# A planner's numbers in a Strassen-like MoE kernel: landing time of two weight loads, rank of the reads of one PSUM bank

## The chip, the core and the metric

The kernel runs on one core of a Trainium2 chip. The metric is the device time of one execution in microseconds. Before the change, three runs took 2589.47, 2592.99 and 2593.93 us; the median is 2592.99 us.

## The reference

Sixteen sequences of 256 tokens with 256 features go through a mixture of experts with a residual. All is float32.

```python
# x (16, 256, 256); E = 8 experts, D = 256, F = 1024; p (16, 8) gating, s (16,) shared gate
g = einsum('bsd,edf->ebsf', x, Wg)
u = einsum('bsd,edf->ebsf', x, Wu)
expert_outs = einsum('ebsf,efd->ebsd', silu(g) * u, Wd)
expert_output = einsum('be,ebsd->bsd', p, expert_outs)
shared = einsum('bsf,fd->bsd', silu(x @ Sg) * (x @ Su), Sd)
out = x + (1 - s) * expert_output + s * shared
```

Every token goes through every expert: the gating only weighs. The shared expert is treated as a ninth one.

## The kernel before

The work is cut into 72 units: nine experts, two halves of the hidden size F, and four groups `g` of four sequences each. Units follow one another with the group as the inner loop, so a half of an expert's weights serves four units in a row, and new weights are needed once in four units.

A unit has two parts. `unit_up` makes gate and up projections with fewer multiplications than the plain product: four sequences and four chunks of weights are combined. For each of the two matrices (m = 0 gate, m = 1 up) there are "diagonal" products, made by `diagonal`, and six "off-diagonal" ones, made by `offdiagonal`. `unit_down` makes the down projection of the unit from seven products in PSUM banks `dn`, and adds them to DRAM tensors `total` through accumulating DMAs that POOL issues (L743). The `h` sums that those products read are made by the helper `sum_` in `unit_down`: two or three on DVE, and one, o3 = `a[0,0] - a[1,0]`, on POOL.

The steps of `diagonal`, on the single PSUM bank D: two matmuls (`ps`), a copy of the bank to `p_` on ACT (L536), two more matmuls into the same bank (`qs`), two DVE subtractions `q_ = bank - p_` (the reads of the bank, shown as `pq<-D,pq`), and then `consume`: for the gate an ACT silu into `sg` (L607), for the up matrix a DVE multiplication into `h` (`h<-D,coef,sg`, L273). Only then is the bank free for the next diagonal.

The steps of `offdiagonal`: POOL makes `s` from `p_` and `q_` (`s<-pq,pq`), TensorE makes one product in a bank M, DVE adds both and so seeds both halves of a bank X (`X<-M,s`), TensorE adds two products to it (`X<-xp,wp`), and gate or up consumes it. There are three X banks, two M banks, three `s` tiles.

Weights: `load_base` loads 256 KB and again 256 KB of gate or up weights into one tile `wb` (two halves, `u` and `v`), and then makes in its second half combinations of the two: two on POOL (`wb<-wb`, L268), one on DVE (L273). `make_pair` makes from them the tiles `wp` on POOL and DVE. There are four `wb` tiles, two of which each half of an expert needs.

Other inputs: in the first four units, `make_xd` and `make_xp` transpose and combine x into tiles `xd` and `xp` and keep them in DRAM; later units load them from there on SP's queue. In the last units, `finish` combines the `total` parts, transposes them back (L829), adds x and stores.

What sets the order. Nothing is written down in the order in which it runs. Each step is given to a `Plan` with an engine, an estimated length, a rank, its predecessors, and a `lag`: how long after its end others can use the result (0.25 where nothing else is given). `Plan.run` goes through a planned time: on each engine it takes, of the steps whose predecessors have ended and lagged, the one of the lowest rank that can have its buffers; TensorE alone must keep to the rank order. It also hands out the buffers, from a queue of free ones per kind, in planned time. When all is planned, the steps are emitted in that order, and the tile layer below builds the program for each engine's queue from it, with the semaphores. Ranks are counted in units of W = 12 per unit of work; r0 is the rank at which a unit starts.

A load's lag is 3 + KB/150 us unless it is given. For `load_base`, `lag` is given except in the first unit (rank below 0): that is line L291, and `u` and `v` both have it, `v` being planned after `u`. The down weights have 12 as well; they are not touched.

Of the kernel before, what the change touches and what calls it, by code (L numbers as in the profile page):

```python
# [46 lines left out]
class Plan:  # L47
# [18 lines left out]
    def add(self, engine, length, rank, emit, deps=(), new=(), uses=(), lag=None):  # L66
        lag = self.HOP if lag is None else lag
        op = Op(engine, length, lag, rank, emit, deps, list(new), list(uses))
        for b in [*op.new, *op.uses]:
            b.users += 1  # L70
        self.ops.append(op)
        return op
# [77 lines left out]
def kernel(  # L150
# [72 lines left out]
    def act(n):  # L223
        return 0.13 + n * 0.0009
# [38 lines left out]
    def load(rank, dst, src, kb, deps=(), new=(), uses=(), lag=None):  # L263
        return add("SP", 0.6, rank, lambda: nc.sync.dma_start(dst(), src), deps, new, uses, lag=lag or 3 + kb / 150)  # L264

    def tt(engine, rank, o, a, b, op, n, deps, new=(), uses=(), slow=1.0):
        eng, length = (nc.vector, dve(n) * slow) if engine == "DVE" else (nc.gpsimd, pool(n))
        return add(engine, length, rank, lambda: eng.tensor_tensor(o(), a(), b(), op), deps, new, uses)  # L268

    def stt(rank, o, a, c, b, op, n, deps, new=(), uses=(), more=0.0):  # L270
        return add(
            "DVE", dve(n, True) + more, rank,
            lambda: nc.vector.scalar_tensor_tensor(o(), a(), c() if callable(c) else c, b(), ALU.mult, op),  # L273
            deps, new, uses,
        )


    def sources(e):
        return (Wg[e], Wu[e], Wd[e]) if e < E else (Sg, Su, Sd)
# [5 lines left out]
    def load_base(m, e, half, rank):  # L285
        b = Buf("wb", f"wb_{m}_{e}_{half}")
        src = [
            sources(e)[m][ts(part, P), ts(half, 4 * P)].rearrange("p (c q) -> p c q", q=P)
            for part in range(2)
        ]  # L290
        lag = None if rank < 0 else 12  # L291
        u = load(rank, lambda: b[:, :, 0, :], src[0], 256, [], [b], lag=lag)
        v = load(rank, lambda: b[:, :, 1, :], src[1], 256, [u], [], [b], lag=lag)
        ops = []
        for i, t in enumerate(POINTS):
            r, x_ = (lambda i=i: b[:, i, 1, :]), (lambda i=i: b[:, i, 0, :])
            if t == 0:
                op = v
            elif abs(t) == 1:
                op = tt("POOL", rank + 1, r, r, x_, ALU.add if t > 0 else ALU.subtract, P, [u, v], uses=[b])  # L300
            else:
                op = stt(rank + 1, r, x_, float(t), r, ALU.add, P, [u, v], uses=[b])
            ops.append(op)
        base[m, e, half], baseop[m, e, half] = b, (u, ops)
# [201 lines left out]
    def mm(length, rank, o, w, mv, start, stop, onto, deps, new=(), uses=()):  # L506
        return add(
            "PE", length, rank,
            lambda: nc.tensor.matmul(o(), w(), mv(), start=start, stop=stop, skip_group_check=onto),  # L509
            deps, new, uses,  # L510
        )
# [3 lines left out]
    def diagonal(n, m, unit, a, rank, pq, consume):  # L515

        e, half, g = unit
        w, (u, rops) = base[m, e, half], baseop[m, e, half]
        xb, xo = xd[g, a], xdop[g, a]
        name = f"{m}_{n}_{a}"  # L520
        bank = Buf("D", f"D_{name}")
        p_, q_ = pq
        new = a == 0
        ps, qs = [], []
        for h, i in enumerate((2 * a + 1, 2 * a)):
            ps.append(
                mm(
                    MM, rank + 1 / 8 + h / 100, lambda h=h: bank[:, h, :], lambda i=i: w[:, i, 0, :],
                    lambda i=i: xb[:, i % 2, :], h == 0, True, h == 1, [u, xo[i][0], *ps],
                    [bank] if h == 0 else [], [w, xb] if h == 0 else [w, xb, bank],  # L530
                )
            )

        sp = add(
            "ACT", act(2 * TB), rank + 0.3,
            lambda: nc.scalar.copy(p_[:, 2 - 2 * a : 4 - 2 * a, :], bank[:, :, :]), ps,  # L536
            [p_] if new else [], [bank] if new else [bank, p_],
        )
        for h, i in enumerate((2 * a + 1, 2 * a)):
            qs.append(  # L540
                mm(
                    MM, rank + 9 / 8 + h / 100, lambda h=h: bank[:, h, :], lambda i=i: w[:, i, 1, :],
                    lambda i=i: xb[:, 2 + i % 2, :], False, True, True, [rops[i], xo[i][1], sp],
                    [], [w, xb, bank],
                )
            )
        ops = {}
        for h, i in enumerate((2 * a + 1, 2 * a)):
            first = new and h == 0
            ops[i] = tt(  # L550
                "DVE", rank + 1.5, lambda i=i: q_[:, i, :], lambda h=h: bank[:, h, :],
                lambda i=i: p_[:, 3 - i, :], ALU.subtract, TB, [*qs, *ops.values()],
                [q_] if first else [], [bank, p_] if first else [bank, p_, q_],
            )
        consume(bank, [*ops.values()], rank + 1.6, [(2 * a + 1, 2 * a + 1), (2 * a, 2 * a)])
        return ops

    def offdiagonal(n, m, unit, k, rank, pq, pqops, consume):
# [31 lines left out]
    def unit_up(n, unit):  # L590
# [70 lines left out]
        for d in range(4):  # L661
            a, m = d // 2, d % 2
            pqops[m].update(
                diagonal(n, m, unit, a, r0 - W + 3 * d, pqs[m], (gate, mult)[m](f"d{a}"))
            )
# [215 lines left out]
    for n, unit in enumerate(units):  # L881
        e, half, g = unit
        r0 = W * n
        if g == 0:
            for m in range(2):
                load_base(m, e, half, r0 - W + 3 * m - (8 if n else 4))
                if n == 0 and m == 0:
                    first_raw = load_raw(-12.5)
            for k in range(len(PAIRS)):
                for m in range(2):  # L890
                    make_pair(m, e, half, k, r0 + 2 * k + m - (8 if n else -4))
            load_down(e, half, r0 + W - 8)
# [63 lines left out]
```

## Time and profile before

| what | value |
|---|---|
| median of three runs | 2592.99 us |
| the profiled execution | 2590.57 us |
| its span in the profile | 2588.8 us |
| granted TensorE clock, mean | 0.997 |
| TensorE busy | 2525.8 us, 98% |
| VectorE (DVE), GpSimd (POOL), ScalarE (ACT) busy | 1846.1, 1800.1, 788.8 us |
| DMA | 421.47 MB, 163 GB/s |
| chain that ended last: TensorE, DMA, DVE | 88%, 6%, 3% of the span |
| wb loads of Wg, issue to landing (median, 33 of them) | 5.5 us |

How to read it. Times are microseconds from the start of the span. A row of a timeline has start, duration, engine, line, operation and tiles (written tile first); in brackets is how long the engine stood idle ahead of it, and what ended that. A row of the waits has who waited for whom: total, times, longest. Almost all operations are recorded through helpers, so that one line (L268 for two-input adds, L273 for multiply-adds, L509 for matmuls) stands for many steps; the tiles tell them apart. TensorE's busy time has modelled ends.

### The profile page before, as it was taken

To read this page: it belongs to the slowest core of one execution; us is meant where nothing else is said; L and a number is where in the kernel's file an instruction comes from. 1 tells how busy PE (TensorE), PEld (TensorE's weight loads), DVE (VectorE), ACT (ScalarE), POOL (GpSimd) and SP (SyncE) were. 2 spreads that over 40 slices of the span, in tenths; PEclk is the share of its full clock that TensorE was granted. 3 is DMA by queue.
4 is the path that set the end of the run, shared out by engine and by line. 5 is a ranking of instruction groups with operands and counts; after the bars stand their busy time and mean duration, and the time that the engine had idled before them with its cause. 6 is when DMAs were issued, how large, how long until landed. Compare 5 with 4: busy or idle time off the path is not lost.

```text
span 2588.8 us, 30164 instructions
## 1 busy us (share of the span) xinstructions
PE 2525.8 (98%) x9644; PEld 1819.9 (70%) x9644; DVE 1846.1 (71%) x3272; ACT 788.8 (30%) x1367; POOL 1800.1 (70%) x1638
## 2 busy tenths in 40 slices
PE   8899999999999999999999999999999999999998
PEld 4667777767776777777676767777776777677766
DVE  6886766777676767676677767676766667776797
ACT  2333333333333333333333333333332333333310
POOL 5686767667676767676766757686767677676654
PEclk9999999999999999999999999999999999999999
DMA  6545666656666656666665665665666666666652
GB/s 196 197 162 154 171 157 164 162 158 164 166 157 164 157 158 169 154 170 156 163 161 161 161 166 157 167 154 158 171 154 164 161 165 158 163 163 177 174 188 90
DMA packets 179087, 421.47 MB, mean 163 GB/s; under 512 B 15057, under 2 KB 84193, under 8 KB 170225
## 3 DMA queue, kind: packets, MB, share of 16 engines
q1 hardware_dynamic: 159280, 294.70, 34.4%
q0 software_dynamic: 19648, 124.86, 26.2%
q8 instruction: 75, 1.23, 0.2%
q14 instruction: 84, 0.68, 0.1%
HBM read 276.90 MB, written 142.61 MB: 162 GB/s over the span
## 4 chain that ended last, share of the span: by engine, by line
PE 88%; DMA 6%; DVE 3%; issue 1%; POOL 1%; SPq 0%; ACT 0%; DVEq 0%; POOLq 0%
PE dn L509 31%; PE X L509 27%; PE D L509 17%; PE M L509 14%; DMA wb<-in_L_cond_Wg_dram 4%; DVE h L273 1%; DMA wb<-in_L_cond_Sg_dram 1%; DVE X L268 1%; DVE h L268 1%; SPq L264 0%; DMA total<-ev 0%; POOL wp L268 0%; PE dn L829 0%; DVE xp L268 0%; DMA wb<-in_L_cond_Wu_dram 0%
## 5 line engine op out<-in xcount | busy, mean ns | idle before, releaser
L268 POOL TENSOR_TENSOR s<-pq,pq 128x512 f32<-128x512 f32 x852 | 1191.3, 1402 | 483.2 <-DVE X L268 471.8
L509 PE MATMUL dn<-h,wd 128*128 128x512 f32 x1988 | 1018.0, 594 | 1.4 <-DVE xd L273 1.4
L509 PE MATMUL X<-xp,wp 128*128 128x256 f32 x3408 | 878.2, 380 | 37.0 <-DVE X L268 37.0
L268 DVE TENSOR_TENSOR X<-M,s 128x512 f32<-128x512 f32 x852 | 586.7, 692 | 435.4 <-PE M L509 227.9
L509 PEld LDWEIGHTS X<-xp,wp 128*128 128x128 f32 x3408 | 645.7, 190 | 254.5 <-issue 103.4
L509 PE MATMUL D<-xd,wb 128*128 128x256 f32 x2272 | 584.5, 380 | 2.6 <-ACT pq L536 2.2
L509 PEld LDWEIGHTS M<-xp,wp 128*128 128x128 f32 x1704 | 324.4, 190 | 346.0 <-issue 338.2
L509 PE MATMUL M<-xp,wp 128*128 128x256 f32 x1704 | 508.1, 380 | 0.1
L729 ACT COPY ev<-dn 128x512 f32<-128x512 f32 x476 | 278.8, 586 | 708.6 <-PE dn L509 708.6
L509 PEld LDWEIGHTS D<-xd,wb 128*128 128x128 f32 x2272 | 431.5, 190 | 67.3 <-ACT pq L536 3.9
L273 DVE SCALAR_TENSOR_TENSOR h<-X,coef,sg 128x256 f32<-128x256 f32 x852 | 375.9, 475 | 122.2 <-PE X L509 107.8
L268 DVE TENSOR_TENSOR h<-h,h 128x512 f32<-128x512 f32 x426 | 448.0, 1052 | 1.9
L509 PEld LDWEIGHTS dn<-h,wd 128*128 128x128 f32 x1988 | 377.6, 190 | 54.8 <-DVE xd L273 2.2
L607 ACT ACTIVATE sg<-X 128x512 f32<-128x512 f32 x434 | 259.1, 597 | 441.8 <-PE X L509 278.0
L536 ACT COPY pq<-D 128x512 f32<-128x512 f32 x284 | 166.5, 586 | 501.7 <-PE D L509 498.3
L268 DVE TENSOR_TENSOR pq<-D,pq 128x256 f32<-128x256 f32 x568 | 218.9, 416 | 25.5 <-PE D L509 25.3
L268 POOL TENSOR_TENSOR h<-h,h 128x512 f32<-128x512 f32 x142 | 197.8, 1393 | 3.6 <-DVE h L268 2.9
L743 POOL DMA_DIRECT2D total<-ev x128 | 112.8, 881 | 66.4 <-ACT ev L729 63.7
L268 POOL TENSOR_TENSOR wb<-wb 128x128 f32<-128x128 f32 x72 | 48.5, 684 | 129.1 <-DMA wb<-in_L_cond_Wg_dram 98.0
L273 DVE SCALAR_TENSOR_TENSOR h<-D,coef,sg 128x256 f32<-128x256 f32 x284 | 134.8, 475 | 0.0
L273 DVE SCALAR_TENSOR_TENSOR wp<-wb,wp 128x256 f32<-128x256 f32 x108 | 106.6, 998 | 29.9 <-POOL wp L268 24.0
L607 ACT ACTIVATE sg<-D 128x512 f32<-128x512 f32 x142 | 84.4, 594 | 98.5 <-DVE pq L268 98.5
(68 smaller groups left out, 561.1 us busy)
## 6 DMA issues: line engine op xcount, KB each, us to landing
xp<-keep_p SPq DMA_DIRECT2D x408, 384.0 KB, 3.9
total<-ev POOLq DMA_DIRECT2D x68, 1024.0 KB, 7.9
xd<-keep_d SPq DMA_DIRECT2D x136, 512.0 KB, 3.5
total<-ev POOLq DMA_DIRECT2D x68, 768.0 KB, 6.9
keep_p<-xp SPq DMA_DIRECT2D x24, 384.0 KB, 2.7
wb<-in_L_cond_Wg_dram SPq DMA_DIRECT2D x33, 256.0 KB, 5.5
wb<-in_L_cond_Wu_dram SPq DMA_DIRECT2D x33, 256.0 KB, 4.2
wd<-in_L_cond_Wd_dram SPq DMA_DIRECT2D x64, 128.0 KB, 2.7
```

The costliest lines, as they stand in the source:

```text
L268: return add(engine, length, rank, lambda: eng.tensor_tensor(o(), a(), b(), op), deps, new, uses)
L273: lambda: nc.vector.scalar_tensor_tensor(o(), a(), c() if callable(c) else c, b(), ALU.mult, op),
L509: lambda: nc.tensor.matmul(o(), w(), mv(), start=start, stop=stop, skip_group_check=onto),
L536: lambda: nc.scalar.copy(p_[:, 2 - 2 * a : 4 - 2 * a, :], bank[:, :, :]), ps,
L607: lambda: nc.scalar.activation(b[:, :, :], bank[:, :, :], AF.Silu), deps, [b], [bank],
L729: lambda ev=ev, at=at, bank=bank: nc.scalar.copy(ev[:, at, :], bank.tile.rearrange("p a t -> p (a t)")),
L743: nc.gpsimd.dma_start(total[g][part], ev[:, 0:k, :], accum_op=ALU.add)
```

## The change

Two numbers of the plan, and the third that follows from the second:

- The lag of the gate and up loads, outside the first unit, is 30 in place of 12.
- In `diagonal`, the two DVE reads of bank D have rank + 0.6 in place of rank + 1.5, and what consumes the bank rank + 0.7 in place of rank + 1.6. A lower rank is taken first.

```diff
@@ load_base
-        lag = None if rank < 0 else 12
+        lag = None if rank < 0 else 30
         u = load(rank, lambda: b[:, :, 0, :], src[0], 256, [], [b], lag=lag)
         v = load(rank, lambda: b[:, :, 1, :], src[1], 256, [u], [], [b], lag=lag)
@@ diagonal
             ops[i] = tt(
-                "DVE", rank + 1.5, lambda i=i: q_[:, i, :], lambda h=h: bank[:, h, :],
+                "DVE", rank + 0.6, lambda i=i: q_[:, i, :], lambda h=h: bank[:, h, :],
                 lambda i=i: p_[:, 3 - i, :], ALU.subtract, TB, [*qs, *ops.values()],
                 [q_] if first else [], [bank, p_] if first else [bank, p_, q_],
             )
-        consume(bank, [*ops.values()], rank + 1.6, [(2 * a + 1, 2 * a + 1), (2 * a, 2 * a)])
+        consume(bank, [*ops.values()], rank + 0.7, [(2 * a + 1, 2 * a + 1), (2 * a, 2 * a)])
```

The computation, the shapes, the buffers and the DMAs are the same; what can differ is the order in the queues and which buffer of its kind a step gets.

## The prediction

> **What bounds the kernel now.** First the page's head and busy times, then a table of three stretches of the span (columns: length, busy time and instructions of PE, PEld, DVE, ACT, POOL, then clock, DMA share, GB/s).
>
> ```profile
> span 2588.8 us, 30164 instructions
> PE 2525.8 (98%) x9644; PEld 1819.9 (70%) x9644; DVE 1846.1 (71%) x3272; ACT 788.8 (30%) x1367; POOL 1800.1 (70%) x1638
> ```
>
> ```profile
> 0.00:160.00 160.00, 139.54 (x504) 89.78 (x505) 123.80 (x216) 46.60 (x92) 108.04 (x127) 0.98 0.57 190
> 160.00:2440.00 2280.00, 2251.57 (x8599) 1633.78 (x8598) 1602.18 (x2862) 720.00 (x1237) 1617.79 (x1459) 1.00 0.62 161
> 2440.00:2588.80 148.80, 134.70 (x545) 96.31 (x543) 120.13 (x196) 22.24 (x38) 74.26 (x54) 1.00 0.50 153
> ```
>
> TensorE is the bound. It idles 20.5 us in the start, 28.4 in the middle, 14.1 in the end: 63 us is all that a new order can win. The waits of the middle stretch, TensorE alone, then two rows of the waits of the whole run (total, times, longest):
>
> ```profile
> PE X L509 <- DVE X L268: 28.4, 15, 2.8
> ```
>
> ```profile
> POOL wb L268 <- DMA wb<-in_L_cond_Wg_dram: 98.0, 13, 11.6
> DVE wb L273 <- DMA wb<-in_L_cond_Wg_dram: 89.6, 15, 7.2
> ```
>
> So the middle has one kind of stall: 15 times, once in four units, 1.1 to 2.8 us. The timeline shows one, POOL and then DVE and PE:
>
> ```profile
> 688.19 1.58 POOL L268 TENSOR_TENSOR s<-pq,pq 128x512 f32<-128x512 f32 x1
> 697.32 0.55 POOL L268 TENSOR_TENSOR wb<-wb 128x128 f32<-128x128 f32 x1 [7.55 <-DMA wb<-in_L_cond_Wg_dram]
> 697.83 1.26 POOL L268 TENSOR_TENSOR s<-pq,pq 128x512 f32<-128x512 f32 x1
> ```
>
> ```profile
> 690.21 0.70 DVE L268 TENSOR_TENSOR X<-M,s 128x512 f32<-128x512 f32 x1 [1.38 <-POOL s L268]
> 697.26 0.29 DVE L273 SCALAR_TENSOR_TENSOR wb<-wb 128x128 f32<-128x128 f32 x1 [6.35 <-DMA wb<-in_L_cond_Wg_dram]
> ```
>
> ```profile
> 699.00 1.13 PE L509 MATMUL X<-xp,wp 128*128 128x256 f32 x4 [1.99 <-DVE X L268]
> ```
>
> The load of the second half of a weight tile is issued at 688.00, when the last diagonal matmul on that tile has read it, and lands 9.2 us later. Work on the tile stands in the queues of POOL and DVE ahead of `s` and of the seed of bank X. Both engines stand still, and TensorE runs out of seeds.
>
> [...]POOL sat 7.55 us before `wb` with an `s` behind it. [...]here issue and wait are 9 us apart on a landing of 9.2 us. [...]DVE's `h<-h` of 128x512 takes 1052 ns on average, the same add with one PSUM input (`X<-M,s`) 692. A swapped POOL instruction can thus cost or save DVE some tenths.
>
> **The change, part by part.** Both edits only alter numbers that the planner sorts by; no operation, byte or wait comes or goes. So I laid the two built programs side by side, instruction by instruction, matched by what they compute and dated by the trace of before. What has moved decides.
>
> Longer landing (L291). Taken alone it moves, of all instructions, only POOL's sum `h<-h` (o3 of L660), by one place, once in four units. The `wb` work on POOL and DVE, the pairs made from it and the weight loads on SP keep their places. A landing time in the plan is not an instruction's place in the built queue: the layer that builds the program evidently sorts once more. Hence the 15 stalls stay: 0 of 28.4 us is won. The swapped sum costs nothing:
>
> ```profile
> 212.39 0.57 POOL L741 DMA_DIRECT2D total<-ev  x1
> 213.70 1.63 POOL L268 TENSOR_TENSOR s<-pq,pq 128x512 f32<-128x512 f32 x1 [0.74 <-DVE X L268]
> 215.29 1.27 POOL L268 TENSOR_TENSOR h<-h,h 128x512 f32<-128x512 f32 x1
> ```
>
> POOL idled 0.74 us before this `s`; the sum's input was ready (DVE had it at 211.3), so it can begin at 212.96 and end at 214.23: `s` is 0.53 us late here, 0.85 in most of the 16 places and 1.37 at worst. The seed reads that `s` 4.8 to 5.0 us after its end: hidden. Without that cover it would be 16 x 0.85 = 14 us. Store and weight sums around it only come earlier or stay.
>
> Lower rank of the reads of bank D (L551, L555). Alone, it moves 26 instructions on DVE, 5 on PE, 4 on POOL, 4 on ACT, 5 issues on SP; every one lies before 160 or after 2440 us. In the middle the D reads already stood as early as their operands allow.
>
> Buffers change hands too: 590 pairs "DVE writes `h` after TensorE has read it" are new in the middle. The tightest leaves 4.1 us by the times of before. No new wait: 0.
>
> Start. (a) A pair of D matmuls at 74.08 waited 1.17 us for ACT's copy (73.44), and that for a POOL `xp` (72.64) behind an `s` of 1.45 us. The `xp` now goes first: copy near 72.05, D near 72.7. X matmuls of 0.86 us that were ahead of D now follow, so what comes next starts near 74.4, not 75.05: -0.6. (b) The seed of X1 (77.31) moves three places back behind `xp` work and ends near 80.3; its matmuls, then due at 79.6, start at 80.35, not 80.21: the gain is gone. (c) Here:
>
> ```profile
> 82.40 0.42 ACT L482 ACTIVATE xp<-xp 128x256 f32<-128x256 f32 x1 [1.84 <-DVE xp L268]
> 82.72 0.57 ACT L536 COPY pq<-D 128x512 f32<-128x512 f32 x1
> ```
>
> ```profile
> 83.34 1.13 PE L509 MATMUL D<-xd,wb 128*128 128x256 f32 x4 [0.81 <-ACT pq L536]
> ```
>
> DVE's `xp` (81.42) is one place earlier, so ACT is free sooner, and D starts near 82.7: -0.65 us. It is kept, since DVE waits for PE at 89 and 94 us. Bounds: if (b)'s delay is not made up, +1.0; if (a) is kept as well, -2.1.
>
> End. (d) Two D reads (0.74 us together) go ahead of the seed that PE waited for at 2500.36: +0.8, but PE's next wait, 1.07 us at 2503.85, is for DVE work behind the same instructions: hidden, +0.8 if not. (e) A sum `h<-h` goes back ten places and uncovers `xd<-dn`:
>
> ```profile
> 2507.51 2.35 DVE L268 TENSOR_TENSOR h<-h,h 128x512 f32<-128x512 f32 x2
> 2509.78 0.68 DVE L268 TENSOR_TENSOR xd<-dn,xd 128x512 f32<-128x512 f32 x1
> ```
>
> ```profile
> 2510.51 1.25 PE L829 MATMUL dn<-ident,wb 128*128 128x128 f32 x8 [1.09 <-DVE xd L268]
> ```
>
> One sum (1.76 us) leaves, one `ev<-dn` (0.68) comes ahead: `xd<-dn` starts 1.06 earlier and takes PE's whole wait. `xd<-dn` for the next bank then comes at 2511.1, so the next `dn` matmul is 0.9 early. PE runs unbroken to 2540 in both: -0.9. Bounds +0.8 to -2.6 (both waits of 1.54 and 1.09 gone).
>
> Sum: -0.65 - 0.9 = -1.55, say -1.5. The profiled execution took 2590.57 us (2588.8 of span, 1.8 around it), so 2589.1 for it. It lies 2.4 us under the median of the runs, 2592.99; the same step from that gives 2591.5.
>
> **Rivals.**
> 1. The change does what its words say: `wb` work moves behind the landing and the 28.4 us go; 2592.99 - 28.4 = 2564.6. For it: the stall is just what a longer landing should cure. Against: no `wb` instruction has moved.
> 2. Start and end win more. They hold 34.6 us of idle TensorE; if the reorder frees a third, 11.5 us go: 2581.5. For it: 18 of the 26 DVE moves lie in the start, where PE loses most. Against: (a) is eaten by (b), (d) costs.
> 3. Slower: the landings at the 15 stalls come later, by a POOL whose accumulating stores (1024 KB) now collide otherwise with the weight loads. They take 8.3 to 10 us in the chain of before and the stalls 1.1 to 2.8, microsecond for microsecond; all at the longest, 15 x 2.8 = 42, which is +13.6: 2606.6. It decides once they average over 9.4 us (15 x 0.35 = 5.2). Against: the swap is 60 us before a stall, and POOL has been idle in between.
>
> **How the numbers follow.** Forecast, about -1.5: 0.83. Rival 1: 0.02, rival 2: 0.09, rival 3: 0.06. The forecast's own spread: runs of before reach from 2589.5 to 2593.9, the bounds add -3 and +3; so 2586 to 2596, which leaves out rivals 1 and 3, most of 2 and 0.04 of the forecast itself. 0.2% is 5.2 us, about what a measurement here can tell from no change. Faster by more: rivals 1 and 2 and 0.02 of the forecast, 0.13; slower by more: rival 3 less its small cases, 0.05; within: 0.82.
>
> **What would show it.** Right: in the middle TensorE still waits 15 times for DVE's X, 25 to 32 us, and POOL and DVE still wait some 100 and 90 us for `Wg`; `s` follows `h<-h` near 214; PE's wait at 83 is gone or short, that at 2510 under 0.3 us, that at 2500 over 2. Wrong: fewer than 10 such stalls in the middle, or new waits of TensorE for anything but a seed there.

## The result and the profile after

The changed kernel takes 2620.88 us (median of four runs, 2615.78 to 2621.21), the kernel before 2593.46 us (2589.47 to 2595.14). The ratio is 1.0103, with a 95% interval of 1.0086 to 1.0121: some 27 us slower. The prediction said 2591.5 and gave a loss of more than its range a chance of 0.05. The profiled execution of the changed kernel took 2620.78 us, its span 2619.0.

The three stretches of the span after, in the columns of the table of before (length, busy time and instructions of PE, PEld, DVE, ACT, POOL, then clock, DMA share, GB/s):

```profile
0.00:160.00 160.00, 140.27 (x505) 90.19 (x506) 123.20 (x216) 46.54 (x92) 108.08 (x127) 0.98 0.57 190
160.00:2440.00 2280.00, 2229.73 (x8475) 1608.54 (x8474) 1641.93 (x2823) 708.20 (x1220) 1593.37 (x1442) 1.00 0.61 159
2440.00:2619.00 179.00, 166.31 (x667) 119.50 (x665) 141.40 (x235) 32.27 (x55) 95.38 (x69) 1.00 0.51 154
```

The start has not changed much. In the middle, a stretch of the same length, TensorE is busy 2229.73 us where it was 2251.57, while DVE is busier (1641.93, was 1602.18) with fewer instructions done. The waits of TensorE in the middle (total, times, longest):

```profile
PE X L509 <- DVE X L268: 43.2, 31, 3.5
PE D L509 <- ACT sg L607: 7.0, 16, 0.4
```

Fifteen waits for a seed have become 31, and there is a kind that was not there: 16 waits for ACT's `sg` ahead of bank D. The stall at new weights is still there, as the waits of the whole run show:

```profile
POOL wb L268 <- DMA wb<-in_L_cond_Wg_dram: 108.7, 14, 11.9
DVE wb L273 <- DMA wb<-in_L_cond_Wg_dram: 92.8, 15, 7.8
```

DVE's extra time sits in one group, the sums `h<-h`. Here is its row (instructions, then busy time and mean ns of one, then idle time before them) after, and then before:

```profile
L268 DVE TENSOR_TENSOR h<-h,h 128x512 f32<-128x512 f32 x426 | 511.4, 1201 | 1.9
```

```profile
L268 DVE TENSOR_TENSOR h<-h,h 128x512 f32<-128x512 f32 x426 | 448.0, 1052 | 1.9
```

63 us more for the same 426 sums. They are not all a little slower: 16 of them, once in four units from 213 to 2347 us, take 3.9 to 4.7 us, most of them 4.19. The timeline shows one, POOL and DVE first and then who is late (start, duration):

```profile
637.21 0.88 POOL L743 DMA_DIRECT2D total<-ev  x1
637.83 1.57 POOL L268 TENSOR_TENSOR h<-h,h 128x512 f32<-128x512 f32 x1
638.34 4.19 DVE L268 TENSOR_TENSOR h<-h,h 128x512 f32<-128x512 f32 x1
639.06 1.56 POOL L268 TENSOR_TENSOR s<-pq,pq 128x512 f32<-128x512 f32 x1
640.28 1.70 POOL L268 TENSOR_TENSOR wd<-wd 128x256 f32<-128x256 f32 x2
642.85 0.68 DVE L268 TENSOR_TENSOR X<-M,s 128x512 f32<-128x512 f32 x1
643.59 1.13 PE L509 MATMUL X<-xp,wp 128*128 128x256 f32 x4 [0.73 <-DVE X L268]
645.80 0.60 ACT L607 ACTIVATE sg<-D 128x512 f32<-128x512 f32 x1 [4.41 <-DVE pq L268]
646.45 1.13 PE L509 MATMUL D<-xd,wb 128*128 128x256 f32 x4 [0.44 <-ACT sg L607]
```

The same place before:

```profile
632.79 0.88 POOL L743 DMA_DIRECT2D total<-ev  x1
633.91 0.68 DVE L268 TENSOR_TENSOR h<-h,h 128x512 f32<-128x512 f32 x1
634.09 1.63 POOL L268 TENSOR_TENSOR s<-pq,pq 128x512 f32<-128x512 f32 x1 [0.43 <-DVE X L268]
635.68 1.26 POOL L268 TENSOR_TENSOR h<-h,h 128x512 f32<-128x512 f32 x1
```

Before, POOL stood idle for 0.43 us behind its DMA issue, because `s` waited for DVE, and DVE's sum began in that gap, at 633.91, and took 0.68 us. After, the swapped sum needs no wait and starts straight behind the issue. DVE's sum, 0.5 us later, does not end before POOL has gone through `h`, `s` and two `wd`, at 641.98: it ends at 642.53. ("Kept out" stands below for just this: DVE's row lasts until POOL's run has ended.) The seed of X and the reads of bank D start behind it on DVE, at 642.85 and 643.84. The same TensorE matmuls start 4.43 us later than before ahead of this place and 6.14 us later behind it: 1.7 us lost, of which the trace counts 0.73 + 0.44 as idle time; the rest stands in TensorE's busy time, whose ends are modelled. Sixteen places of 1.7 us make some 27 us.

### The profile page after: what moved, and what is told of

The parts are those of the page before. It is cut to its first block, busy times and chain, and to the rows that moved or that the text cites. A ratio compares the mean times of both kernels' runs of the same rounds, so it can differ in the third digit from the quotient of the medians.

```text
span 2619.0 us, 30161 instructions
## 1 busy us (share of the span) xinstructions
PE 2536.3 (97%) x9644; PEld 1818.2 (69%) x9644; DVE 1906.5 (73%) x3272; ACT 787.0 (30%) x1367; POOL 1796.8 (69%) x1638
## 4 chain that ended last, share of the span: by engine, by line
PE 86%; DMA 5%; DVE 5%; issue 3%; POOL 1%; ACT 0%; SPq 0%; DVEq 0%; POOLq 0%; ACTq 0%
PE dn L509 29%; PE X L509 26%; PE D L509 18%; PE M L509 13%; DMA wb<-in_L_cond_Wg_dram 4%; DVE h L273 1%; DVE h L268 1%; DVE X L268 1%; DMA wb<-in_L_cond_Sg_dram 1%; DVE pq L268 1%; POOL wp L268 0%; ACT sg L607 0%; SPq L264 0%; DMA keep_p<-xp 0%; PE dn L829 0%
## 5 line engine op out<-in xcount | busy, mean ns | idle before, releaser
L268 DVE TENSOR_TENSOR h<-h,h 128x512 f32<-128x512 f32 x426 | 511.4, 1201 | 1.9
L268 DVE TENSOR_TENSOR pq<-D,pq 128x256 f32<-128x256 f32 x568 | 218.7, 416 | 25.8 <-PE D L509 25.5
L268 POOL TENSOR_TENSOR h<-h,h 128x512 f32<-128x512 f32 x142 | 209.9, 1479 | 2.0 <-DVE h L268 1.3
L273 DVE SCALAR_TENSOR_TENSOR wp<-wb,wp 128x256 f32<-128x256 f32 x108 | 106.4, 995 | 30.1 <-POOL wp L268 24.1
```

## The experiments

Two questions: which part of the change does it, and why DVE's sum takes so long in these places. Elsewhere it is short beside POOL's work as well: the `h<-h` at 644.17 in the changed kernel took 1.26 us and ended 0.55 us behind the POOL `s` that it started beside (644.88), while POOL went on. In the middle of the changed kernel no sum `h<-h` of DVE but these 16 takes more than 1.65 us. The last column is the ratio to the kernel before on the same chip, with its interval.

| kernel | long DVE sums in the middle | us, median | ratio |
|---|---|---|---|
| e1, lag alone | 15 of 4.2 us; group mean 1192 ns | 2630.26 | 1.0137 (1.0112 to 1.0162) |
| e2, rank alone | none; mean 1053 | 2592.77 | 1.0000 (0.9989 to 1.0010) |
| e3, whole change, sum put back | none; mean 1051 | 2592.72 | 0.9994 (0.9981 to 1.0006) |
| e4, before, swap by hand | 16 of 4.2; mean 1200 | 2629.92 | 1.0143 (1.0122 to 1.0164) |
| e5, issue behind the sum | 16 of 4.4, at another sum | 2620.57 | 1.0105 (1.0084 to 1.0126) |
| e6, wd later | 16, most of them 2.8 | 2602.38 | 1.0032 (1.0018 to 1.0047) |
| e7, issue ahead elsewhere | 15 of 3.4 | 2614.82 | 1.0080 (1.0062 to 1.0098) |
| e9, wb sums held | none | 2559.92 | 0.9885 (0.9867 to 0.9904) |
| e10, the change, all mended | none | 2549.65 | 0.9841 (0.9824 to 0.9859) |
| e12, as e10 without the rank | none | 2557.56 | 0.9864 (0.9840 to 0.9888) |

**Which part.** e1 is the first hunk of the change alone, e2 the two others. e3 and e4 change only the list of steps just before it is emitted (`mark` is a name given to the sum o3, to `s` and to the issue of `total`):

```diff
 # e3, in the changed kernel; e4 in the kernel before, with i > j and order.insert(i, order.pop(j))
+        for n in range(5, 66, 4):
+            at = {op.mark: i for i, op in enumerate(order) if op.mark}
+            i, j = at["sum", n - 1, 0], at["s", 1, n, 1]
+            if i < j:
+                order.insert(j, order.pop(i))
         for op in order:
             op.emit()
```

> Only the longer landing time; in the built program 15 POOL sums stand one place earlier than before and nothing else has moved. Theory (each swapped sum lets a DVE sum of 4.2 us in place of 0.68 us in behind it, 1.7 us of TensorE each): 15 x 1.7 = 25.5 us more than before, about 2619 us, with 15 such DVE sums more than before has. Rival A (the lower rank of the reads of bank D makes the loss): within 3 us of before, no long DVE sums.

> Only the lower rank. Theory: start and end alone differ, -1.5 us as the prediction's steps had it, 2590 to 2593 us, one long DVE sum (the one near 141 us that before has too). Rival A: about +27 us, 2620.

> The changed kernel whole, but in 16 units the POOL sum is put back behind the s it had passed; the rest of the built program is the changed one's. Theory: as rank alone, 2590 to 2593 us, the 16 long DVE sums gone. Rival B (the loss comes from where buffers and weight loads fall under the longer landing time, the swap is only its sign): stays near 2620 us.

> The kernel before, with nothing but that swap made by hand in 16 units. Theory: 16 x 1.7 = 27 us more than before, about 2620 us, 16 DVE sums of 4.2 us more. Rivals A and B: within 3 us of before.

All four fall on the side that the theory named, e2 and e3 within its range, e1 and e4 above it. The swap alone makes the loss, in a kernel with the old landing time (e4), and putting 16 sums back takes it away under the new one (e3). Rivals A and B are out. e1 and e4 lose some 35 us by their medians, more than the 25.5 and 27 expected and than the change itself; the interval of e1 overlaps that of the change (1.0112 to 1.0121), the one of e4 just misses it. A lower granted clock goes with it: 0.991 to 0.995 in the four runs of e1 and 0.992 to 0.995 in those of e4, against 0.995 to 0.998 in the runs of before beside them. The profiled execution of e4 has a span 10.6 us longer than that of the changed kernel (2629.6 and 2619.0); for the same matmuls TensorE is busy 8.4 us longer in it (2544.7 and 2536.3 us), at a clock of 0.993 against 0.997. That the clock is all of the excess is not shown. The row of the sums in e4:

```profile
L274 DVE TENSOR_TENSOR h<-h,h 128x512 f32<-128x512 f32 x426 | 510.8, 1200 | 1.9
```

**Why so long.** Two guesses. H1: a run of POOL sums that starts right behind POOL's DMA issue keeps DVE's sum out until POOL idles. H2: any dense run does, and the issue stands there by chance. e5 and e7 move the issue, e6 shortens the run. Each uses a rule on the emitted list as above, and an edge that keeps the moved step behind another in POOL's queue without a wait. In short:

```diff
 # e5, in the changed kernel, i being the issue of total ahead of the sum
+            order[i].behind = order[j].mark            # j: the s behind the sum
+            order.insert(j, order.pop(i))
 # e6, in the changed kernel, i being two steps wd
+            order[i].behind = ("s", 0, n, 2)           # the s after next
 # e7, in the kernel before, other units: range(6, 66, 4)
+            order[i].behind = ("s", 1, n, 1)           # issue behind s ...
+            order[s].behind = order[i].mark            # ... and the sum behind it
```

> The changed kernel, with POOL's DMA issue of total moved from directly ahead of the swapped sum to three places behind it (POOL: h, wd, s, total) in 16 units; the sum stays swapped and nothing on the other engines moves. Theory H1 (a run of POOL sums that begins right behind POOL's DMA issue, without a gap, keeps a DVE sum of two SBUF inputs out until POOL idles): the 16 long DVE sums are 1.5 us or less, the time falls back to 2588 to 2600 us. Theory H2 (any dense run of POOL sums keeps DVE out, the issue is chance): the 16 stay near 4 us, 2615 to 2625 us.

> The changed kernel, with two wd differences taken out of the run behind the swapped sum in 16 units: POOL has total, h, s, and then an s that must wait for DVE, so that it idles after 2.8 us in place of 4.2. If DVE's sum waits until POOL idles (H1 and H2 alike): the 16 DVE sums take 2.4 to 3.0 us in place of 4.2, and the loss shrinks from 1.7 us each to 0.5 or less: 2592 to 2602 us. If the long sum is a fixed penalty: they stay at 4.2 us, 2615 to 2625.

> The kernel before, with no sum swapped; in 15 other units (which have a run of h, s, h, s that DVE today gets into at each border, 1.2 to 1.4 us) the DMA issue of total is put directly ahead of that run. H1: one DVE sum in each of the 15 takes 4 to 7 us, and the time grows by 25 to 60 us. H2: no long DVE sum comes, within 5 us of before.

e5 missed its time and says more for it. The sums at the old place fell to 1.15 us, as H1 has it; but the long wait came back behind the issue's new place, at a sum that took 0.88 us before:

```profile
1355.26 0.86 POOL L766 DMA_DIRECT2D total<-ev  x1
1356.12 4.43 DVE L287 TENSOR_TENSOR h<-h,h 128x512 f32<-128x512 f32 x1
```

Behind the issue POOL has `s`, `wd`, `h`, `wd` without a gap until 1360.0, and DVE's sum ends at 1360.55. In e5 the long sum went with the issue, not with the swapped sum. In e6 the 16 sums end when POOL runs out of work after `h` and `s`: 2.83 us in most, within the 2.4 to 3.0 expected, but 3.35 in one, and the loss falls to 8.7 us by the medians, just over what was expected (0.5 us a place). A fixed penalty is out. In e7 a run beside which DVE's sums had taken 1.2 to 1.4 us keeps one out for 3.39 us once the issue stands ahead:

```profile
1247.60 0.89 POOL L768 DMA_DIRECT2D total<-ev  x1
1248.17 3.39 DVE L289 TENSOR_TENSOR h<-h,h 128x512 f32<-128x512 f32 x1
```

That is 15 times. It is less than the 4 to 7 us expected, and the cost, 21 us, is below the 25 to 60: the next POOL `h` needs what DVE is making and waits 0.70 us for it, so the run ends itself after two instructions.

e8 and e11 measure the long sum by itself, and compute nothing else: a start sign from ACT, then POOL's steps and DVE's, four times each. In short, without the options of the single cases:

```diff
+ first = nc.gpsimd.dma_start(d, ev, accum_op=ALU.add)      # cases with an issue
+ for n in range(4):                                        # 8 in c and i
+     nc.gpsimd.tensor_tensor(po[n], a, pb, ALU.add)        # 128x512, both in SBUF
+ nc.vector.tensor_tensor(dl[n], ps, go, ALU.add)           # DVE's lead, so that the next falls into POOL's first
+ nc.vector.tensor_tensor(do, da, db, ALU.add)              # the measured sum
```

> Nothing of the reference is computed: nine cases, four times each, of POOL sums 128x512 of two SBUF inputs back to back, into which a DVE sum of the same form falls 0.4 to 0.7 us after the first one's start. Case a: 4 sums with no DMA issue ahead; i: 8 such; b: accumulating issue directly ahead, 4 sums; c: the same with 8; d: plain store ahead; e: as b, but DVE's sum has one PSUM input; f: as b with a pause of over 1 us between issue and sums; g: the issue is SP's; h: as b, DVE's sum falls into the issue itself. H1: a, i, f, g take 1.4 us or less, b and d 4 to 5, c 9 to 10, e 0.7. H2: a like b, near 4 to 5, and i like c, near 9 to 10.

> Nothing of the reference is computed: six cases, four times each. b: as before, accumulating issue, 4 POOL sums, a DVE sum falls into the first: 5.7 us. j: over 1 us of pause between issue and sums, and the DVE sum later, so that it falls into the first POOL sum: if the pause ends the hold, 1.3; if not, 5.7. k: a memset of 128x1 between issue and sums: 1.3 if any other instruction ends the hold, 5.7 if only idling does. l: DVE's instruction is a copy of one SBUF input: 0.7 or less if only two inputs are kept out[...]. m: an issue of 32 KB in place of 1 MB: 5.7 if the size does not matter. n: POOL must wait for ScalarE after two of its four sums: near 3.2 if DVE gets in when POOL idles.

| case | ahead of POOL's sums | DVE's instruction | us |
|---|---|---|---|
| a, i | nothing; 4 and 8 sums | two SBUF inputs | 1.3, 1.3 |
| g | an issue on SP's queue, 0.1 us behind the start of POOL's first | two SBUF inputs | 1.3 |
| b, c | POOL's accumulating issue; 4 and 8 sums | two SBUF inputs | 5.7, 10.5 |
| d | POOL's plain store | two SBUF inputs | 5.4 |
| m | accumulating issue of 32 KB, not 1 MB | two SBUF inputs | 5.7 |
| k | issue, then a memset of 128x1 | two SBUF inputs | 5.7 |
| h | issue; DVE's sum falls into it | two SBUF inputs | 6.2 |
| n | issue; POOL waits after two sums | two SBUF inputs | 3.2 |
| j | issue, then a pause of 0.19 us | two SBUF inputs | 1.5 |
| e | issue | one input in PSUM | 0.7 |
| l | issue | copy, one SBUF input | 5.4 |

The four rounds of a case agree within 0.25 us. The cases b, c and d lie 0.4 to 0.7 us above the ranges expected for them; in b DVE ends 0.56 us behind POOL's last sum. Case f missed its aim: DVE's sum fell into the issue and was over before POOL's first sum began (0.68); j repeats it with the sum later. Case a and case b, the second time round:

```profile
221.62 1.26 POOL L81 TENSOR_TENSOR po<-go,pb 128x512 f32<-128x512 f32 x1 [12.00 <-ACT go L60]
222.12 1.31 DVE L90 TENSOR_TENSOR do<-da,db 128x512 f32<-128x512 f32 x1
...
241.97 0.87 POOL L70 DMA_DIRECT2D d_b<-ev  x1 [14.97 <-ACT ev L69]
242.09 0.68 DVE L88 COPY dl<-ps 128x512 f32<-128x512 f32 x1
242.58 1.56 POOL L79 TENSOR_TENSOR po<-go,pb 128x512 f32<-128x512 f32 x1
242.69 5.65 DVE L90 TENSOR_TENSOR do<-da,db 128x512 f32<-128x512 f32 x1
```

In a DVE's sum ends at 223.43, 0.55 us after POOL's first (222.88); in b it ends 0.56 us after POOL's fourth, at 248.34. H2 is out: beside 8 sums without an issue DVE's took 1.3 us (i), beside 8 behind an issue 10.5 (c).

**What the stall at the weights was worth.** The prediction read the 28.4 us as `wb` work queued too early. In e9, e10 and e12 each `wb` sum keeps, in the built queue, its place behind the step that the planner emitted ahead of it on its engine (cut; `last` has that step for POOL and DVE):

```diff
+            if op.mark == "hold" and op.engine in last:
+                with self.tc.issue_after(last[op.engine].ins):
+                    op.emit()
```

> The kernel before with one thing added: the built program keeps the sums on freshly loaded gate and up weights in the place where the planner wrote them, 11 to 20 places later on POOL and 31 to 46 on DVE than they stood; nothing else moves, and the landing time in the plan stays 12. If the 28.4 us of idle TensorE in the middle come from wb work queued too early, as the prediction read it, they go: 2560 to 2570 us. If the weights are what TensorE waits for: within 4 us of before.

> The changed kernel (both edits) with the sum put back behind s and the wb sums kept in the planner's place, which under the longer landing time is 38 to 40 places later on POOL and 73 to 83 on DVE. Here the landing time reaches the built program. Theory: no long DVE sum and no stall at the weights: 2558 to 2570 us; with the weights' work piled up elsewhere instead: 2575 to 2600.

> As e10 (longer landing time, sum put back, wb sums kept in the planner's place), without the lower rank of the reads of bank D. If the rank makes the 10 us by which e10 lies below e9, this comes out where e9 did, 0.987 to 0.990 of before; if the later place of the wb sums makes them, where e10 did, 0.982 to 0.986.

In e9 TensorE has one wait left in the middle, of 0.4 us:

```profile
160.00:2440.00 2280.00, 2279.11 (x8710) 1653.39 (x8710) 1679.28 (x2903) 729.65 (x1252) 1635.28 (x1478) 1.00 0.62 165
```

30.5 us are won by the medians, where 28.4 stood in the profile; 2559.92 us is just under the range expected. e10, with the sum put back as well, is the fastest version here, below both kernels: 0.9841 of before. Its 2549.65 us lie 8 us under the range expected. In it the longer landing time at last moves what its words name. Whether the rank makes the 10 us between e9 and e10 is not settled: without it, e12 lies between them, and its interval reaches both. For the rank speaks that TensorE's idle time in the first 160 us is 15.6 us in e10 and 21.0 in e12, while the middle has 2.0 and 2.2.

## Why the prediction was wrong

**The built program.** Right. That the landing time alone moves only POOL's sum held: in the traces of e1 and of before, DVE, ACT, TensorE and SP have the same order, and POOL's differs in 15 sums. (The sum stands at L694; the L660 of the prediction is a slip.) The stall at the weights stayed, 15 times, with 31.1 us of idle TensorE for 28.4. One reading was wrong without harm: the load's issue and the wait for it are not 9 us apart. POOL began to wait 1.8 us behind the issue, and the wait ended with the landing.

**"The swapped sum costs nothing."** This step failed. It looked at one thing only, who reads the `s` that the sum delays, and that cover was there: 5 us of slack. It did not look at DVE, whose sum had begun in the 0.43 us gap that the swap closed. The term put at 0 measured some 27 us, 1.7 in each of 16 places (e3 and e4 show that it is this term).

**"Some tenths."** That a swapped POOL sum can cost or save DVE some tenths of a us was the author's estimate, from the means of two groups: 1052 ns for `h<-h`, 692 for the same add with one input in PSUM. Cases a and i agree with it (1.3 us, against 0.68 for the short sums of the trace of before). Behind POOL's DMA issue it does not hold: DVE's sum lasted through four POOL sums (5.7 us) and eight (10.5). The size could have been bounded from the trace of before. Inside an issue of `total` one `h<-h` of DVE took 4.61 us in place of 0.68:

```profile
140.90 0.57 POOL L741 DMA_DIRECT2D total<-ev  x1
141.02 4.61 DVE L268 TENSOR_TENSOR h<-h,h 128x512 f32<-128x512 f32 x1
```

By this row a sum near an issue took 3.9 us longer; 16 of them would have given an estimate of 63 us for the upper end, not 0.

**Rival 3** was on the right side with the wrong mechanism: the stalls at the weights cost some 3 us more idle time, not 13.6, and the 27 came from elsewhere.

**Start and end.** Most single steps came. The D pair stood at 72.74 (72.7 predicted) and the later D at 82.21 (82.7), and the transposes at 2540.63 had no wait left, so that the delay of TensorE's matmuls fell there from 31.2 to 30.1 us; 1.06 was worked out. Two did not: the X matmuls of step (b) came at 79.73, so the gain of (a) was not lost there, and the wait that was to grow over 2 us at 2500 was 1.56. How much the start won in sum can't be read from one execution: at the sums that before has at 210.64 us, the changed kernel is 0.2 us early, e2 0.7 early, and e1, whose order is that of before up to there, 1.2 late. e2, the rank alone, is within 0.1% of before, which agrees with this sum of -1.5 us and would agree with no gain as well.

**The sign that was named** fired: "new waits of TensorE for anything but a seed" are the 16 for `sg`.

## What to carry to other kernels

When a POOL instruction moves, look not only at who reads its result but at what DVE does beside it at that moment: here it was a sum of 0.68 us that became one of 4.19. Where a DMA issue on POOL stands ahead of a run of POOL sums, look in the trace for DVE sums that last as long as the run. What shortened them in these runs was a pause between issue and run (0.19 us in case j: 1.5 us in place of 5.7) and a wait of POOL inside the run (case n: 3.2; e6: 2.83 in place of 4.19). An issue at the end of a run, where POOL then idles, is not among these runs; in e5, where the next run followed straight behind, moving the issue did not help (16 sums of 4.4 us). Bound such a cost by the longest row of its group, not by the mean: the trace of before had a single sum of 4.61 us among sums of 0.68, and the change made 16 of 3.9 to 4.7. A planner's number is worth something only if the built queue keeps the order that it made.

## What the runs showed of the hardware that was not expected

In cases b and c, behind a DMA issue on POOL's own queue, a gapless run of POOL sums kept DVE's sum out to its end (5.7 us for four, 10.5 for eight). With 32 KB moved in place of 1 MB (m) it took 5.7, with a memset between (k) 5.7, with a plain store (d) 5.4. With an issue on SP's queue beside the sums (g) it took 1.3, and with a pause of POOL 1.5 (j) and 3.2 (n). The pause of j was 0.19 us. In the kernel before, at 2036.42, the `s` behind the issue started at 2037.20, 0.09 us after DVE's seed of X had ended and 0.10 us ahead of the issue's end, where the run at 637.83 and the one of case b, which kept DVE out, start 0.26 ahead; DVE's sums beside it took 0.68 and 1.28 us.

A DVE copy with one SBUF input was kept out as well (l, 5.4), a sum with one input in PSUM not (e, 0.68). What becomes of a sum that starts inside the issue is not settled. In h, 0.13 us into the issue, it took 6.2 us. The sum at 141.02 above, 0.12 us into it, took 4.61 and ended at 145.63, 0.55 us behind the first of two `wp` sums of POOL and ahead of the second's end. But in f, 0.20 us into the issue with a pause of POOL behind, it took 0.68, and in the kernel before at 124.67, 0.23 us into it with `s` straight behind, 0.41 for half the size.

Why these sums last so long is not shown by these runs. An early start of POOL's sums does not explain it: they start 0.3 us early behind an accumulating issue (1.56 us the first) and not behind a plain store (1.27), and DVE's sum is long in both (b, 5.7; d, 5.4; and in the changed kernel 3.88 us at 213.32, where POOL's run starts at 212.79, 0.02 us after the end of a plain store's issue).
